# Adding and norming the experts' output earlier in an attention layer, its additions in halves, and zeros written by ScalarE

## The chip, the cores and the metric

The kernel runs on one core of a Trainium2 chip. A core has four engines that compute: TensorE (PE, matrix products into PSUM), VectorE (DVE), ScalarE (ACT, activation functions) and GpSimd (POOL). SyncE (SP) issues most of the transfers. Each engine works through its own queue in order, and semaphores tie the queues together. The metric is device time in microseconds (us); less is better.

## The reference

The whole program is a stack of eight layers on an input of 8 sequences of 512 positions by 256 features. Each layer is added to the residual stream as a normed output of a normed input:

```python
x = x + _layernorm(_L1_ffn_ref(_layernorm(x, axis=-1), ...), axis=-1)
x = x + _layernorm(_L2_attn_ref(_layernorm(x, axis=-1), ...), axis=-1)
```

The fourth layer, `_L1_ffn_ref`, is a mixture of 48 experts whose weighted outputs are scatter-added into one array. The fifth, `_L2_attn_ref`, is the third mixer of the stack and the place of the change. It is causal attention with 16 heads of 16 features, with a Silu on its three projections and q and k scaled by their norms:

```python
def _L2_attn_ref(x, Wq, Wk, Wv, Wo, q_scale, k_scale):
    q = jax.nn.silu(x @ Wq.T); k = jax.nn.silu(x @ Wk.T); v = jax.nn.silu(x @ Wv.T)
    ...
    r_q = jnp.linalg.norm(q, axis=-1, keepdims=True)
    r_k = jnp.linalg.norm(k, axis=-1, keepdims=True)
    q_dir = q / (r_q + EPS)
    k_dir = k / (r_k + EPS)
    scores = jnp.einsum('bhnd,bhmd->bhnm', q_dir, k_dir)
    scores = scores * (r_q * sq) * (jnp.swapaxes(r_k, -2, -1) * sk)
    scores = jnp.where(mask, scores, -jnp.inf)
    probs = jax.nn.softmax(scores, axis=-1)
    out = jnp.einsum('bhnm,bhmd->bhnd', probs, v)
    return out.transpose(0, 2, 1, 3).reshape(B, N, D) @ Wo.T
```

## The kernel before

The residual stream X stays in SBUF for the whole program, as a tile of 128 partitions by 4 blocks of 256 for each sequence. Everything is in 32-bit floats. A scheduler places the instructions, within each engine's queue, by the order of the program and by when it expects each to be ready. So an instruction can stand in its queue earlier than its place in the source.

The third mixer is `l2_attn`. It works on quads: a quad is four heads of one sequence, so a sequence has four. The main loop takes one turn for each of the 32 quads. A turn has two halves. In the first, `maxima` makes the scores S of the next quad (L1386) and DVE takes the greatest of each row (L1391, the group `junk`). These become one more column of q through a transpose (`ptm`) and an addition (L1400). In the second half, `weigh` makes the transposed scores T of this quad (L1421), ScalarE takes their Exp (L1424, into `PT`), POOL sets the upper triangle of the diagonal block to zero (L1426, `affine_select`, called the causal fill below), and PE multiplies by v (L1411, `o`). At the end `strip` transposes the q of the quad after next (`ptq`), and ScalarE and DVE copy it by turns into `qz`. One DVE copy (`OS`, L1435) and `spread` bring the output back into `O`.

Two further pieces of work hang on the sequences. `finish(b-1)` multiplies by Wo (L190), norms the product (`add_norm`, L164 on) and adds it to X; it is issued in the first turn of the next sequence. `front(b+1)` prepares the next sequence and is a generator which the loop advances by steps, four in each of the first two turns and up to twelve in the later ones. Its steps are, in this order:

- `late`: it loads the experts' output of that sequence from DRAM (`yl`, L1263), takes statistics on DVE, norms it on ScalarE (L177, `yn`) and adds it to X on POOL (L179, one addition of 128 x 1024);
- the norm of X (`lnst`, `lnmv`, `xn` L133), its transposes (`pxT`, L146; copied to `xT`, L148) and the first of four projections: q and k (`pqk`, L1317), v (`pv`, L1324), their Silus (L1321, L1327), the squares on POOL (L1330) and their sums on DVE (L1331);
- the second, third and fourth projection, one for each step;
- the norms of q and k: a chain of small DVE operations (L90 to L96, L1335 to L1341) whose result is `f`;
- the scaling of q and k by `f` on POOL (L1345, four instructions);
- four transposes of k (`ptk`, L1359) with their copies to `KT` (L1351).

Before the loop, front 0 runs by itself, and `maxima` of the first quad follows it. Several tiles hold zeros in places that are never written again: `qkp` (128 x 4096), `va` and `qz` (128 x 2048) and `mx` (128 x 512), each in two buffers. POOL writes them at the beginning (L1301 to L1306), with minus one and one in two narrow columns.

Silu and Exp belong to different tables of ScalarE. A change from one to the other is an instruction of its own in the trace (ACT_TABLE_LOAD). The tiles `yl` and `xn` share one buffer of the pool `s1`, so a load of `yl` can only start once the previous `xn` has been transposed. The PSUM pool for projections and transposes has two buffers, that for S and T has five.

## Time and profile before

| | us |
|---|---|
| median of 3 runs | 5200.95 (5196.74 to 5203.29) |
| profiled execution | 5193.12 |
| its span, first to last instruction | 5191.4 |
| third mixer, about | 2005 to 3085 |
| one of its sequences | 132.5 |

Inside the mixer, the engines' idle time before some groups of one sequence (window 2272 to 2404.5), with what ended it:

| group | idle before it, us | ended by |
|---|---|---|
| PE o, L1411 | 5.7 | POOL causal fill |
| PE pxT, L146 | 3.8 | DVE xn |
| PE S, L1386 | 2.7 | DVE maxima, ACT and DVE qz |
| PE ptk, L1359 | 1.7 | POOL scaling of q and k |
| PE T, L1421 | 1.7 | ACT Exp |

A timeline row has the start, the length (both in us), the engine, the line, the operation with output and inputs, the shape and the count; a bracket tells how long the engine stood idle before it and what ended that. A matrix product in 32-bit floats shows as two records. In a row of groups the numbers after the bar are busy time and the mean in ns, then the idle time before the group.

### The profile page before, as it was taken

What the parts mean: (1) busy time and instruction counts of PE and PEld (TensorE: products, weight loads), DVE (VectorE), ACT (ScalarE), POOL (GpSimd) and SP (SyncE); (2) the same over time, 40 slices, a digit from 0 to 9 for tenths busy, and PEclk for the clock granted to TensorE, in tenths of its full rate; (3) what the DMA queues carried; (4) which work ended last, traced back from release to release, by engine and by line L of the source; (5) the groups of instructions that cost most, each with busy time, mean ns of one, the idle gap of its engine ahead of it and who ended that gap; (6) DMA issues with size and microseconds to landing.
All of it is one profiled execution on the core that took longest, in us unless ns stands there. A gap on an engine that the chain in (4) does not pass through costs nothing.

```text
span 5191.4 us, 56559 instructions
## 1 busy us (share of the span) xinstructions
PE 4407.5 (85%) x18804; PEld 2700.6 (52%) x18804; DVE 3047.7 (59%) x8229; ACT 1928.3 (37%) x3817; POOL 1865.3 (36%) x1201
## 2 busy tenths in 40 slices
PE   8745789999983996988888899988888888899998
PEld 3334675565552894544444455533333333368885
DVE  7999646466687113555555653357778877761115
ACT  5401323434341332433333333355555555321112
POOL 0001213444342343111111110057889887803331
PEclk9876899999996997999999999999999999899999
DMA  4397411000001893000000000011111111126763
GB/s 113 80 208 176 132 47 48 5 5 9 5 17 42 225 253 97 5 5 5 5 5 5 1 20 1 0 43 42 45 45 49 45 43 43 47 80 216 227 214 101
DMA packets 401528, 357.89 MB, mean 69 GB/s; under 512 B 209394, under 2 KB 334020, under 8 KB 400676
## 3 DMA queue, kind: packets, MB, share of 16 engines
q1 hardware_dynamic: 373236, 305.83, 21.2%
q0 software_dynamic: 16320, 31.65, 2.2%
q10 hardware_dynamic: 11680, 16.80, 1.0%
q8 instruction: 149, 2.44, 0.2%
q14 instruction: 143, 1.17, 0.1%
HBM read 287.87 MB, written 66.09 MB: 68 GB/s over the span
## 4 chain that ended last, share of the span: by engine, by line
PE 34%; DVE 18%; issue 6%; POOL 5%; ACT 3%; DMA 1%; DVEq 0%; POOLq 0%; ACTq 0%; SPq 0%
DVE h L1706 7%; PE gb L1785 4%; PE T L1421 4%; PE h L1240 3%; DVE junk L1391 3%; PE g L1534 3%; PE y L1677 3%; PE yb L1799 2%; DVE dB L1652 2%; PE py L190 2%; PE pc L1599 2%; PE y L1251 2%; POOL h L1709 2%; PE o L1411 1%; PE pi L1585 1%
## 5 line engine op out<-in xcount | busy, mean ns | idle before, releaser
L1709 POOL TENSOR_TENSOR h<-h,C 128x1024 f32<-128x1024 f32 x256 | 596.2, 2357 | 178.2 <-DVE h L1706 140.0
L1677 PE MATMUL y<-h,C 128*128 128x512 f32 x1024 | 530.9, 659 | 104.6 <-POOL h L1709 104.6
L1706 DVE TENSOR_TENSOR_SCAN h<-dA,dB 128x512 f32<-128x512 f32 x512 | 589.4, 1204 | 29.4 <-ACT dA L1703 11.7
L1703 ACT ACTIVATE dA<-dl,A 128x512 f32<-128x512 f32 x512 | 352.5, 691 | 411.4 <-DVE h L1706 410.8
L935 POOL TENSOR_SCALAR p<-p,rs 128x128 f32<-128x128 f32 (+3 forms) x256 | 276.3, 1088 | 385.6 <-DVE rs L934 226.0
L1677 PEld LDWEIGHTS y<-h,C 128*128 128x128 f32 x1024 | 201.0, 207 | 410.9 <-issue 222.0
L1424 ACT ACTIVATE PT<-T 128x256 f32<-128x256 f32 (+3 forms) x512 | 208.5, 438 | 416.4 <-PE T L1421 409.8
L179 POOL TENSOR_TENSOR X<-X,yn 128x1024 f32<-128x1024 f32 x64 | 151.2, 2363 | 559.8 <-ACT yn L177 483.2
L1386 PE MATMUL S<-KT,qz 128*128 128x512 f32 (+3 forms) x1024 | 321.2, 453 | 22.4 <-DVE mx L1391 8.7
L1421 PE MATMUL T<-qz,KT 128*128 128x512 f32 (+3 forms) x1024 | 320.4, 445 | 12.0 <-ACT PT L1424 9.3
L1426 POOL TENSOR_SCALAR_AFFINE_SELECT PT<-PT 128x512 f32<-128x512 f32 x128 | 81.1, 637 | 609.8 <-ACT PT L1424 609.8
L1657 POOL TENSOR_TENSOR dB<-du,B 128x2048 f32<-128x2048 f32 x64 | 289.8, 4529 | 0.1
L1391 DVE CUSTOM_DVE_ANT_0 junk<-S,mask 128x256 f32<-128x256 f32 (+3 forms) x512 | 251.4, 491 | 61.9 <-PE S L1386 4.9
L1785 PE MATMUL gb<-xbT,w_b 128*128 128x256 f32 (+1 forms) x1472 | 255.3, 332 | 1.0 <-ACT ts L1989 0.6
L1386 PEld LDWEIGHTS S<-KT,qz 128*128 128x128 f32 x1024 | 180.4, 191 | 142.4 <-DVE mx L1391 30.7
L1652 DVE TENSOR_TENSOR dB<-du,pb 128x2048 f32<-128x2048 f32 x64 | 145.5, 2275 | 170.2 <-PE pb L1649 120.3
L1785 PEld LDWEIGHTS gb<-xbT,w_b 128*128 128x128 f32 x1472 | 230.2, 191 | 23.1 <-ACT ts L1989 0.8
L1791 DVE TENSOR_TENSOR hTb<-sb,gb 128x512 f32<-128x512 f32 x71 | 48.9, 688 | 325.3 <-PE gb L1785 325.3
L1421 PEld LDWEIGHTS T<-qz,KT 128*128 128x128 f32 x1024 | 169.1, 191 | 132.4 <-issue 66.5
L933 ACT ACTIVATE p<-p,nm 128x128 f32<-128x128 f32 (+3 forms) x256 | 143.8, 563 | 198.8 <-DVE nm L929 193.5
L1245 ACT ACTIVATE hT<-h,w_l_ffn 128x128 f32<-128x128 f32 x384 | 109.8, 368 | 220.3 <-PE h L1240 220.3
L1240 PE MATMUL h<-xgT,w 128*128 128x128 f32 x1536 | 185.0, 279 | 0.0
(506 smaller groups left out, 9132.7 us busy)
## 6 DMA issues: line engine op xcount, KB each, us to landing
w_b<-l3f_w SPq DMA_DIRECT2D x138, 512.0 KB
w<-l1f_w SPq DMA_DIRECT2D x48, 1024.0 KB
C<-xdd SPq DMA_DIRECT2D x128, 256.0 KB
B<-xdd SPq DMA_DIRECT2D x64, 256.0 KB
w<-l1f_w SPq DMA_DIRECT2D x48, 256.0 KB
toep<-l0fd SPq DMA_DIRECT2D x32, 320.0 KB
X<-x SPq DMA_DIRECT2D x16, 512.0 KB
toep<-l0fd SPq DMA_DIRECT2D x32, 256.0 KB
```

The costliest lines, as they stand in the source:

```text
L935: nc.gpsimd.tensor_scalar(p[:, 0:n], p[:, 0:n], rs, None, ALU.mult)
L1240: nc.tensor.matmul(ph[:, j, :], lhsT=w1[:, s, c, m * P:(m + 1) * P], rhs=xgT[:, c, :], start=(c == 0), stop=(c == 1))
L1386: nc.tensor.matmul(ps[:, 0:n], lhsT=QZ[:, j, qt * P:n], rhs=KT[:, g, 0:n], start=True, stop=True)
L1391: nc.vector.tensor_tensor_reduce(out=junk[:, 0:n], in0=tiles[j][:, 0:n], in1=mask[:, L - n:L], scale=1.0, scalar=-3.0e38, op0=ALU.add, op1 ...
L1421: nc.tensor.matmul(ps[:, 0:n], lhsT=KT[:, g, kt * P:(kt + 1) * P], rhs=QZ[:, j, kt * P:L], start=True, stop=True)
L1652: nc.vector.tensor_tensor(dB, du, pb[:, None, :].to_broadcast([P, 4, L]), ALU.mult)
L1657: nc.gpsimd.tensor_tensor(dB, du, B[:, None, :].to_broadcast([P, 4, L]), ALU.mult)
L1677: nc.tensor.matmul(py[2 * j + c], lhsT=K.ident, rhs=h[:, c, :], start=False, stop=(n == NS - 1))
L1703: nc.scalar.activation(dA, dl[:, c, :], AF.Exp, scale=A[:, c, n:n + 1])
L1706: nc.vector.tensor_tensor_scan(hs[-1][:, c % 2, :], dA, dB[:, c, :], 0.0, ALU.mult, ALU.add)
L1709: nc.gpsimd.tensor_tensor(h, h, C[:, None, :].to_broadcast([P, 2, L]), ALU.mult)
L1785: nc.tensor.matmul(ps[:, q, :], lhsT=ww[:, k, (c + q) * P:(c + q + 1) * P], rhs=xT[:, k, :], start=(k == 0), stop=(k == 1))
```

## The change

- `add_norm`, `project_out` and `late` can split the addition to X into parts; the third mixer uses two, each over half of the blocks.
- `front` yields once more, between the norm of X and its transposes. All eight fronts are made at the beginning. A new helper `norm_of` runs a front's first two steps, the addition of the experts' output and the norm. It is called for sequence b+2 in the last turn of sequence b; for sequence 1 behind `f` of front 0.
- The steps that the loop takes in each turn stay as they were in number, so with two of them gone ahead, all four projections fall into the first turn, and `f`, the scaling and two transposes of k into the second.
- The zeros are written by ScalarE, as an Identity with scale 0 of one column of the identity matrix, broadcast along the row. Buffer set 0 is done before front 0; set 1 behind the last Silu of front 0. The columns of minus one and one stay on POOL.
- `tc.issue_after(x)` keeps the instructions of its block behind x on x's own engine.

```diff
-    def add_norm(self, b, ys, pool, tag="yn", halves=()):
+    def add_norm(self, b, ys, pool, tag="yn", halves=(), parts=1):
...
-        nc.gpsimd.tensor_tensor(self.X[b], self.X[b], t, ALU.add)
+        m = NT // parts
+        for n in range(0, NT, m):
+            x = self.X[b][:, n:n + m, :]
+            nc.gpsimd.tensor_tensor(x, x, t[:, n:n + m, :], ALU.add)
...
-        K.add_norm(b, [y[:, n, :] for n in range(NT)], pool)
+        K.add_norm(b, [y[:, n, :] for n in range(NT)], pool, parts=2)
...
-        for j in range(2):
-            nc.gpsimd.memset(qkp[j], 0.0)
+        def padding(j):
+            for t in (qkp, va, qz, mx):
+                n = 1
+                for d in t[j].shape[1:]:
+                    n *= d
+                names = " ".join("abc"[:len(t[j].shape) - 1])
+                nc.scalar.activation(
+                    t[j].rearrange(f"p {names} -> p ({names})"),
+                    K.ident[:, 0:1].to_broadcast([P, n]), AF.Identity, scale=0.0)
             nc.gpsimd.memset(qkp[j][:, :, 16:32, 16:17], -1.0)
-            nc.gpsimd.memset(qz[j], 0.0)
-            nc.gpsimd.memset(mx[j], 0.0)
-            nc.gpsimd.memset(va[j], 0.0)
             nc.gpsimd.memset(va[j][:, :, :, 16:17], 1.0)

         def front(b, res):
             QKP, VA = qkp[b % 2], va[b % 2]
             K.late(b, s1)
             yield
-            xT = K.norm_T(b, s1, pmm, "mm")
+            xn = K.norm(b, s1)
+            yield
+            xT = K.norm_T(b, s1, pmm, "mm", xn=xn)
...
-                nc.scalar.activation(
+                res["v"] = nc.scalar.activation(
                     VA[:, n, :, 0:16], pv.rearrange("p (h d) -> p h d", h=16), AF.Silu)
...
-            nc.vector.tensor_tensor(
+            res["f"] = nc.vector.tensor_tensor(
                 f, f, row[:, None, :].to_broadcast([P, NT, 32]), ALU.mult)
...
-                b, [(OT[:, k, :], wo[:, k, :]) for k in range(2)], pmm, "mm", s1, leave=True)
+                b, [(OT[:, k, :], wo[:, k, :]) for k in range(2)], pmm, "mm", s1, leave=True, parts=2)
...
-        for _ in front(0, res[0]):
+        fronts = [front(b, res[b]) for b in range(NB)]
+        def norm_of(b):
+            if b < NB:
+                for _ in range(2):
+                    next(fronts[b])
+        padding(0)
+        for _ in fronts[0]:
             pass
+        with tc.issue_after(res[0]["v"].ins):
+            padding(1)
+        with tc.issue_after(res[0]["f"].ins):
+            norm_of(1)
...
-            if g == 0:
-                nxt = front(b + 1, res[b + 1]) if b + 1 < NB else iter(())
+            nxt = fronts[b + 1] if b + 1 < NB else iter(())
...
             for _ in range(4 if g < 2 else 12):
                 next(nxt, None)
+            if g == 3:
+                norm_of(b + 2)
             done[i] = weigh(b, g, made.pop(i), lambda: strip(i + 2))
```

More of the change, by code (lines that the diff above doesn't have):

```diff
@@ L178, in add_norm, with project_out @@
                 t[:, n, :], ys[n], AF.Identity, bias=nb[:, n:n + 1], scale=r[:, n:n + 1])
-        nc.gpsimd.tensor_tensor(self.X[b], self.X[b], t, ALU.add)
-    def project_out(self, b, chunks, psum, ptag, pool, tag="yn", leave=False):
+        m = NT // parts
+        for n in range(0, NT, m):
+            x = self.X[b][:, n:n + m, :]
+            nc.gpsimd.tensor_tensor(x, x, t[:, n:n + m, :], ALU.add)
+    def project_out(self, b, chunks, psum, ptag, pool, tag="yn", leave=False, parts=1):
         nc = self.nc
@@ L194, in project_out @@
             halves.append(ps)
-        self.add_norm(b, ys, pool, tag, halves if leave else ())
+        self.add_norm(b, ys, pool, tag, halves if leave else (), parts)
 def load_l0_attn(K):
```

## The prediction

> **What bounds the kernel now.** First the page: TensorE (PE) is busy most of the span, but that is a mean over eight layers. The edits lie in the third mixer and in the helper its input goes through.

> ```profile
> PE 4407.5 (85%) x18804; PEld 2700.6 (52%) x18804; DVE 3047.7 (59%) x8229; ACT 1928.3 (37%) x3817; POOL 1865.3 (36%) x1201
> ```

> Then the windows of the mixer (about 2005 to 3085 us). Its sequences repeat every 132.5 us. One such window (columns: window, length, then busy us and count of PE, PEld, DVE, ACT, POOL, clock, DMA):

> ```profile
> 2269.00:2402.00 133.00, 117.33 (x516) 64.84 (x515) 73.92 (x270) 51.90 (x105) 22.96 (x26) 0.95 0.02 5
> ```

> PE is the bound, with 15 us of gaps. The timeline of PE tells where they lie:

> ```profile
> 2343.35 1.98 PE L1421 MATMUL T<-qz,KT 128*128 128x512 f32 x4
> ...
> 2359.00 1.02 PE L1421 MATMUL T<-qz,KT 128*128 128x128 f32 x6 [0.34 <-ACT PT L1424]
> 2361.75 0.64 PE L1411 MATMUL o<-PT,va 128*32 128x256 f32 x8 [1.73 <-POOL PT L1426]
> 2366.29 0.66 PE L1411 MATMUL o<-PT,va 128*32 128x128 f32 x8 [3.89 <-POOL PT L1426]
> 2370.77 2.19 PE L146 MATMUL pxT<-C,xn 128*128 128x128 f32 x8 [3.83 <-DVE xn L133]
> ...
> 2383.89 1.12 PE L1386 MATMUL S<-KT,qz 128*128 128x512 f32 x2
> ...
> 2415.53 1.12 PE L1386 MATMUL S<-KT,qz 128*128 128x512 f32 x2 [0.26 <-ACT qz L1374]
> ```

> Taking the first S product of a turn as its start, the four turns of a sequence last 51.2, 31.6, 25.6 and 24.0 us (2332.69, 2383.89, 2415.53; then by the period from 2283.09, 2308.68). The last turn carries no front and is dense. The first turn carries the finish, the late addition and most of a front: its second half (T products on) is 40.5 us, 2343.35 to 2383.89. In it POOL's causal fills stand behind two whole additions to X (2358.76 and 2363.30, 2.35 us each), and the front's transposes wait for POOL X, then 4.6 us of DVE statistics. The second turn holds the fourth projection; its Silu falls among Exps:

> ```profile
> 2397.09 1.28 ACT L1321 ACT_TABLE_LOAD   x1
> 2398.64 0.60 ACT L1321 ACTIVATE qkp<-pqk 128x512 f32<-128x512 f32 x1 [0.27 <-PE pqk L1317]
> 2399.26 1.28 ACT L1424 ACT_TABLE_LOAD   x1
> 2400.55 0.60 ACT L1424 ACTIVATE PT<-T 128x512 f32<-128x512 f32 x1
> ```

> Last the beginning of the mixer, where nothing covers a wait:

> ```profile
> 2010.54 10.40 DVE L118 TENSOR_SCALAR onv<-onmv 128x4 f32<-128x4 f32 x1
> 2020.98 0.17 DVE L90 TENSOR_SCALAR ony<-onv 128x4 int32<-128x4 int32 x1
> ```

> A four-element instruction shown as 10.4 us ends as POOL's last large memset does (2019.12 + 1.80).

> **The change, part by part.** The built order of the changed kernel's instructions gives the queues; durations are the trace's.

> *Start.* Six large memsets and two small leave POOL. ScalarE's zeros of buffer set 0 cost, by the nearest long row,

> ```profile
> L1604 ACT ACTIVATE u<-u 128x2048 f32<-128x2048 f32 x8 | 15.3, 1912 | 0.1
> ```

> 1.91 twice, 3.6 for 4096 elements (1.91 plus 2048 at 0.83 ns, the slope between the 128- and 512-wide Exps) and 0.6: 8.0 us. They can run from 2005.1, when the scatter has landed as for the mask memset, to 2013.1. Behind them on ACT stands yn; its scale is ready at 2013.2 (onv at 2010.5 plus the 2.6 us chain), so they are covered, barely. Gain 10.2. Of X in halves only one addition and two statistics (1.9 us) follow yn instead of 3.9: 2.0 more. The Silu load no longer waits for the second yl (2038.56; free at 2035.4): 2.8. Sequence 1's addition and norm leave the middle of front 0: first Silu to the end of f took 19.5, and takes 3 projections at 2.67 (8.0), Silu, square and sum 2.4, and the undisturbed chain 6.1, together 16.5: 3.0. Set 1's zeros (8.0 again) lie on ACT while DVE and POOL make f and scale qkp (about 10 us). Given back: that yn (2.1) is now ahead of the first S, and the norm's pieces among the first maxima (1.8). Start: 18.0 − 3.9 = **14 us gained**. If the broadcast read made ACT half as fast, both sets would stick out by some 8 and 4: 2 gained. I take 14: L1604 has the same form.

> *First turn.* late(b+2) and its norm are written in the last quad, but the built order puts them right after front b+1's projections; late's SP load still waits for the transposes to free xn, so its position on SP is unchanged. It lands 3.7 us later; behind the DVE instruction that waits for it stand only sums of squares not needed for 15 us. All four projections now lie among the T products. With 0 at 2343.35: as before until the finish's products end at 8.45; transposes, then xT at 11.9. ACT has the finish's scale at 12.3 (0.8 sooner, no yl statistics between), and then runs without a gap: yn 2.05, eight table loads 10.3, four Silu pairs 3.5, ten Exps 3.5, the qz copy 0.6. S can begin at about **32.5**, against 40.5 with three projections. PE's own work there is 29.7, so ACT becomes this stretch's bound, by some 3 us. The halved adds and the fills on POOL are each ready before PE asks. Gain 8.1.

> [...] The row above shows the next instruction 1.29 us after the load's start. [...]

> *Second turn.* Its projection and four loads go, and PE work falls by 2.1. But f's DVE chain, once in an idle stretch, moves in among the maxima, where DVE is the pace (junk every 0.845 us). Small operations fit into the 0.22 us between an accumulator read and the next junk (O's products do today), so I price seven chain steps and three products at about 0.05, the reciprocal 0.7, L1338 0.4, OS 0.5, four statistics 0.14 each: some 2.8, with half a microsecond of late start 3.3. For late's halved adds on POOL, meeting DVE products with two SBUF inputs (one such met today took 0.89 instead of 0.16, at 2043.39), 1.5 more. S half 12.2 + 4.8 = 17.0. The T half like that of the third turn, 13.0, with one transpose fewer and 0.6 of waiting for POOL's qkp: 13.2. Sum 30.2, against 31.6: gain 1.4. Third turn: one transpose fewer, 0.4. The ends for DVE: nothing extra, or all at full busy time (chain 4.5, OS 0.7, statistics 1.65, both adds blocking 2.35: 9.2).

> *Sum.* Six sequences with finish and front: 6 × (8.1 + 1.4 + 0.4) = 59.4. Sequence 0 has no finish to gain from: its T half was already interleaved at 22.9 us and gets one more Silu with two loads and a yn (+4.0); second turn 32.1 to 30.0, third −0.4: net +1.5. Last sequence: nothing. 14 + 59.4 − 1.5 = **72 us**. The profiled execution (5193.12, span 5191.4) would be 5121; it lies 7.8 under the median of the runs, so 5200.95 − 72 = **5129**.

> **Rivals.**

> *DVE gives more back.* If moved steps count at their full busy time, each second turn costs 4.4 more; with sequence 0, 7 × 4.4 = 31: **5160**. For it: DVE is in order and PE's S buffers are five. Against: the O products that already ride there free.

> *Interleaved Silus stall PE (slower).* The second turn today is 31.6 against 25.6 with 1.7 more PE work: 4.3 us lost for one interleaved projection. If each of four costs that, the first turn is 57.2 (24.3 bare, 4.5 finish, 1.0 transposes, 10.3 projections, 17.2 stalls), the sequence 57.2 + 30.2 + 25.2 + 24.0 = 136.6, 4.1 worse; six of them +25, sequence 0 about +15, start −14: +26, **5227**. It decides once the first turn's T half exceeds 42 us. Against: sequence 0's first turn interleaves three with only 0.8 us over its PE work, and part of the 4.3 is waiting for qkp's scaling.

> *Only the start gains*: the turns cancel, 5200.95 − 14 = **5187**. *The change doesn't do what it says*: zeros or halves move but the scheduler keeps the waits, **5199**; the built order speaks against it.

> **How the numbers follow.** Main case 0.62 (its own range 5105 to 5150, from the DVE ends), DVE 0.18, start only 0.07, nothing 0.04, slower 0.09. About 0.2% (10 us) can be told from no change. Faster: 0.62 + 0.18 + 0.07 = 0.87; same 0.04; slower 0.09. The range 5100 to 5186 holds the first two cases and leaves out about 0.2.

> **What would show it.** Right: no 10-us onv; first S about 14 us earlier; PE without 3.9-us gaps before o and pxT; ACT nearly solid in the first turn's T half, eight loads at 1.28; period about 122.5. Wrong: table loads followed by idle ACT, S halves of second turns beyond 17 us, or PE waiting for Silu more than 3 us per sequence.

## The result and the profile after

| | before | changed |
|---|---|---|
| median of the runs shown, us | 5202.12 (5196.74 to 5203.87, 4 runs) | 5108.95 (5105.01 to 5111.53, 4 runs) |
| profiled execution, us (span) | 5193.12 (5191.4) | 5105.01 (5103.3) |
| third mixer, first load of `yl` to the load of `wd`, us | 1083.1 | 994.4 |

The ratio of the times is 0.9822, with a 95% interval of 0.9805 to 0.9839: some 93 us less. In the two profiled executions it is 88.1, and the mixer alone is 88.7 shorter; the layers ahead of it ended 3.8 later in the second execution and those behind took 3.1 less. The code there is the same in both, and in the profiles of the kernels below the mixer's first load lies anywhere from 2004.2 to 2018.2, so both are read as drift. The medians differ by more because the profiled execution before lay 9 us under its median and the changed one 4.

Times of turns below run from the first S product of one turn to that of the next, as in the prediction. Read along the whole mixer they are:

| | before | changed |
|---|---|---|
| first `yl` load to the first S | 63.4 | 46.9 |
| to the second S (the turns begin) | 78.7 | 64.3 |
| sequence 0: its four turns | 35.7, 32.1, 25.4, 24.0 | 38.8, 28.0, 24.9, 24.4 |
| sequences 1 to 6: first turn (mean) | 51.5 | 42.55 |
| second turn (mean) | 31.6 | 29.0 |
| third and fourth turn | 25.5, 24.0 | 25.05, 24.0 |
| last sequence: two turns with a next S | 30.4, 24.3 | 29.9, 24.0 |

The 88.7 us are 14.4 of start, 1.1 in sequence 0, 6 × 12.1 = 72.6 in the six like sequences and 0.5 at the end.

The page's busy times of the changed kernel barely differ from before; only the span does:

```profile
PE 4394.7 (86%) x18804; PEld 2694.8 (53%) x18804; DVE 3045.6 (60%) x8229; ACT 1958.5 (38%) x3835; POOL 1854.5 (36%) x1209
```

ACT has gained 30 us of work (zeros and table loads) and the span is 88 shorter. PE has lost 12.8 us of busy time with the same 18804 matmuls; that is a clue to which the text comes back.

The start, in the timeline of DVE, with the four-element instruction that took 10.40 us before:

```profile
2014.34 0.24 DVE L118 TENSOR_SCALAR onv<-onmv 128x4 f32<-128x4 f32 x1
```

and in that of ACT, the zeros ahead of the first scaling:

```profile
2008.88 3.62 ACT L1310 ACTIVATE qkp<-C 128x4096 f32<-128x4096 f32 x1 [7.18 <-DMA out_d<-yw,iT]
2012.40 1.89 ACT L1310 ACTIVATE va<-C 128x2048 f32<-128x2048 f32 x1
2014.20 1.89 ACT L1310 ACTIVATE qz<-C 128x2048 f32<-128x2048 f32 x1
2016.00 0.61 ACT L1310 ACTIVATE mx<-C 128x512 f32<-128x512 f32 x1
2017.04 1.09 ACT L177 ACTIVATE yn<-yl,onb,ony 128x256 f32<-128x256 f32 x2 [0.42 <-issue]
```

The zeros end at 2016.61 and the scaling follows at 2017.04, when its scale has just been made: covered, with nothing to spare.

The first turn, in the timeline of PE (start, length, what; in brackets the idle time ahead and what ended it):

```profile
2320.73 1.98 PE L1432 MATMUL T<-qz,KT 128*128 128x512 f32 x4
...
2331.34 1.98 PE L1328 MATMUL pqk<-w_l_attn,xT 128*128 128x512 f32 x4
...
2335.40 1.06 PE L1422 MATMUL o<-PT,va 128*32 128x512 f32 x8
...
2347.09 1.98 PE L1328 MATMUL pqk<-w_l_attn,xT 128*128 128x512 f32 x4
...
2352.56 1.12 PE L1397 MATMUL S<-KT,qz 128*128 128x512 f32 x2 [1.47 <-ACT qz L1385]
```

From the first T product to the next S are 31.8 us, where it was 40.5 with a projection fewer. The gaps of 1.73, 3.89 and 3.83 us ahead of o and of the transposes are gone; the only long one left is the 1.47 ahead of S. ACT in the same stretch:

```profile
2333.03 2.07 ACT L177 ACTIVATE yn<-yn,onb,ony 128x256 f32<-128x256 f32 x4 [0.89 <-DVE onb L170]
2335.12 1.28 ACT L1332 ACT_TABLE_LOAD   x1
2336.41 0.60 ACT L1332 ACTIVATE qkp<-pqk 128x512 f32<-128x512 f32 x1
2336.91 0.38 ACT L1338 ACTIVATE va<-pv 128x256 f32<-128x256 f32 x1
2337.30 1.28 ACT L1435 ACT_TABLE_LOAD   x1
2338.60 0.88 ACT L1435 ACTIVATE PT<-T 128x384 f32<-128x384 f32 x2
...
2351.95 0.56 ACT L1385 COPY qz<-ptq 32x512 f32<-32x512 f32 x1
```

The Silu starts 1.29 after its load does, the Exp 1.30 after its own. Eight loads stand here, ACT has no idle time from 2333.03 to 2352.5, and its last piece is the copy to qz for which S waits the 1.47 us. So ACT ends last in this stretch, 1.4 us behind PE, which is busy for 30.4 of the 31.8.

What the prediction had not looked at is the row of the granted clock. By windows (window, length, then busy time and count of PE, PEld, DVE, ACT and POOL, the granted PE clock, DMA share, GB/s), first of the kernel before, in the gaps of its first turn:

```profile
2363.50:2370.80 7.30, 0.69 (x9) 0.24 (x9) 4.67 (x24) 0.37 (x3) 2.73 (x2) 0.50 0.00 0
2370.80:2376.00 5.20, 5.17 (x12) 2.90 (x13) 0.88 (x3) 2.46 (x3) 0.00 (x0) 0.50 0.34 89
```

then of a whole sequence of the changed one:

```profile
2188.10:2309.00 120.90, 113.64 (x514) 62.87 (x513) 76.16 (x266) 54.17 (x106) 23.48 (x29) 1.00 0.02 5
```

Before, the clock is at half in and behind the gaps, 0.50 in both windows, and the front's transposes and first projection take longer: eight transposes 2.19 us and the first q and k product 3.55, in the changed kernel 0.60 for each four and 1.98. Over sequences 1 to 6, each taken from its first S to that of the next sequence, PE is busy for 116.7 us on the mean before and for 113.9 in the changed kernel, with the same matmuls. So of the 12.1 us won per sequence 9.2 are idle time of PE that is gone, and about 2.8 are the same work done at a higher clock (by sequence 0.94 to 0.96 before, 0.99 to 1.00 in the changed kernel). That the waits are what lowered the clock is tested in the last experiment.

### The profile page after: what moved, and what is told of

The parts are those of the page before. It is cut to its first block, busy times and chain, and to the rows that moved or that the text cites. A ratio compares the mean times of both kernels' runs of the same rounds, so it can differ in the third digit from the quotient of the medians.

```text
span 5103.3 us, 56570 instructions
## 1 busy us (share of the span) xinstructions
PE 4394.7 (86%) x18804; PEld 2694.8 (53%) x18804; DVE 3045.6 (60%) x8229; ACT 1958.5 (38%) x3835; POOL 1854.5 (36%) x1209
## 4 chain that ended last, share of the span: by engine, by line
PE 37%; DVE 18%; issue 4%; POOL 4%; ACT 3%; DMA 1%; DVEq 0%; POOLq 0%; ACTq 0%; SPq 0%
DVE h L1730 7%; PE T L1432 5%; PE gb L1809 4%; DVE junk L1402 3%; PE h L1243 3%; PE g L1558 3%; PE y L1701 3%; PE yb L1823 2%; PE py L193 2%; DVE dB L1676 2%; PE pc L1623 2%; PE y L1254 2%; POOL h L1733 2%; PE o L1422 2%; PE pi L1609 1%
## 5 line engine op out<-in xcount | busy, mean ns | idle before, releaser
L1730 DVE TENSOR_TENSOR_SCAN h<-dA,dB 128x512 f32<-128x512 f32 x512 | 589.0, 1203 | 29.4 <-ACT dA L1727 11.7
L182 POOL TENSOR_TENSOR X<-X,yn 128x1024 f32<-128x1024 f32 (+1 forms) x80 | 154.1, 1932 | 590.3 <-ACT yn L177 529.3
```

The source lines that it names most:

```text
L1730: nc.vector.tensor_tensor_scan(hs[-1][:, c % 2, :], dA, dB[:, c, :], 0.0, ALU.mult, ALU.add)
```

## Experiments

Medians are set against the changed kernel's 5108.95 us; each ratio is against the kernel before in the same set of runs. The first three each undo one part.

**The early addition and norm undone**

```diff
             xn = K.norm(b, s1)
-            yield
...
-        with tc.issue_after(res[0]["f"].ins):
-            norm_of(1)
...
-            if g == 3:
-                norm_of(b + 2)
```

> The changed kernel with the early addition and norm undone: both are again the first steps of a front, in the first turn, and the fourth projection falls into the second turn. Zeros by ScalarE and halved additions stay. Theory (the early norm and the regrouped projections carry most of the gain, the start carries about 15 us): the start gains 12 to 15, the halves about 2 us per sequence in the first turn, so 20 to 30 us under the kernel before, about 5175. Rival (the halved additions, by letting the causal fills through, carry the first turn's gain): 70 us or more under the kernel before, below 5135. First turns should stay above 48 us by the theory, near 44 by the rival.

Measured: 5172.43 us, ratio 0.9956 (0.9939 to 0.9973), 63 above the changed kernel. First turns are at 49.9 on the mean again (51.5 before), second turns at 31.64. So the place of this work carries the first and second turns; the halves alone bring 1.6 per first turn. This kernel takes the gathering of the projections back too; the fourth experiment separates the two.

**Additions to X in one piece**

```diff
-        K.add_norm(b, [y[:, n, :] for n in range(NT)], pool, parts=2)
+        K.add_norm(b, [y[:, n, :] for n in range(NT)], pool)
...
-... pmm, "mm", s1, leave=True, parts=2)
+... pmm, "mm", s1, leave=True)
```

> The changed kernel with each addition to X in one piece again. Theory (in the changed kernel the additions lie beside ScalarE's work, and only the start follows one directly): 2 to 5 us slower than the changed kernel, 5111 to 5114, with first turns still near 42.5. Rival (the halves are what keeps the causal fills on time): 3 us or more per sequence, 5130 or above.

Measured: 5116.89, ratio 0.9844 (0.9828 to 0.9861), 8 slower, where 2 to 5 were expected. The first S is 2.5 later and the second 3.7; first turns stay at 42.5, second ones grow by 0.35. With the late addition out of the way, halving the additions pays at the ends of the mixer, not in its turns.

**All zeros by GpSimd at the start**

```diff
-        padding(0)
...
-            padding(1)
+        for j in range(2):
+            nc.gpsimd.memset(qkp[j], 0.0)
...
+            nc.gpsimd.memset(va[j], 0.0)
```

> The changed kernel with all zeros written by POOL at the beginning again. Theory (the start's 10 us are DVE's four-element operation held up by POOL's memsets, and nothing else of the change helps there): 9 to 12 us slower than the changed kernel, about 5119, and the first onv again takes about 10 us. Rival (ScalarE's 8 us only replaced the wait, or the long onv is a recording artefact): within 3 us of the changed kernel.

Measured: 5123.3, ratio 0.9857 (0.9841 to 0.9874), 14.4 slower, more than the 9 to 12 that were expected. The same instruction in DVE's timeline is long again, and it ends as the last memset in POOL's does, at 2025.9:

```profile
2015.59 10.34 DVE L118 TENSOR_SCALAR onv<-onmv 128x4 f32<-128x4 f32 x1
...
2024.11 1.79 POOL L1308 MEMSET va<- 128x2048 f32 x1
```

The first S is 11.7 later. The long row comes and goes with the memsets on GpSimd, and it is no artefact of the recording, since the first S moves with it.

**The fourth projection back in the second turn**

```diff
-            for _ in range(4 if g < 2 else 12):
+            for _ in range((3, 5, 12, 12)[g]):
```

> The changed kernel with three front steps in the first turn and five in the second, so that only the early addition and norm differ from the old placing of the projections. Theory (the early norm opens the first turn; the fourth projection is worth little, since its two loads move with it): first turns near 38.5, second near 32 to 33, the whole within 10 us of the changed kernel on the slow side, 5109 to 5119. Rival (gathering the projections in the first turn is what pays): 4 us or more per sequence, 5135 or above.

Measured: 5132.9, ratio 0.9871 (0.9854 to 0.9887), close to the rival's 5135 and well above the theory's 5119. First turns fall to 38.9, but second turns are 34.3 to 37.2 (32.9 in sequence 6), above the 31.6 of before: f is made late and GpSimd scales behind it, as PE's timeline of this kernel shows:

```profile
2384.77 1.13 PE L1432 MATMUL T<-qz,KT 128*128 128x256 f32 x4 [1.03 <-ACT PT L1435]
...
2389.64 0.69 PE L1370 MATMUL ptk<-C,qkp 128*128 128x128 f32 x2 [2.77 <-POOL qkp L1356]
```

First and second turn together take 83.1 us before, 74.3 here and 71.6 in the changed kernel (means of sequences 1 to 6). So the early addition and norm bring 8.8 us per sequence and the gathering of the projections 2.8; with it the chain of f starts beside the first S of the second turn and not some 19 us later.

**No table loads**

```diff
-                nc.scalar.activation(qk, ps.rearrange(...), AF.Silu)
+                nc.scalar.activation(qk, ps.rearrange(...), AF.Identity)
...
-                    VA[:, n, :, 0:16], pv.rearrange(...), AF.Silu)
+                    VA[:, n, :, 0:16], pv.rearrange(...), AF.Identity)
```

> The Silu of the three projections q, k and v in the third mixer's fronts is left out (they are copied as they are), so that ScalarE has no table loads there; everything else is as in the changed kernel. Theory: eight loads of 1.28 us make ScalarE the bound of the first turn's second half by only 2 to 3 us over TensorE's own work, so without them the first turns fall from 42.5 to about 40, the first turn of sequence 0 falls by 1 to 3, later turns stay; the kernel is 15 to 20 us faster than the changed one (5109), about 5090 to 5095. [...] Second rival: TensorE's own work or the fills on GpSimd end last, and the loads are covered: first turns stay at 42 and the time at 5105 to 5110.

Measured: 5105.22, ratio 0.9815 (0.98 to 0.983): the second rival's numbers. But this run does not tell what it was made to tell. (The kernel leaves Silu out, so only its times are of use.) First turns are 43.1, and the timeline shows why: the scheduler put one of the late addition's scalings between the second and third projection on ACT, presumably since it no longer reckoned with the loads, and there ACT waited 3.66 us for `onb`. Only in sequence 6, which has no late addition, was the first turn 40.35 against 42.84. So the order had to be held:

```diff
-        for n in range(NT):
-            nc.scalar.activation(
+        with self.tc.issue_after(after) if after is not None else ExitStack():
+            for n in range(NT):
+                nc.scalar.activation(
...
-            K.late(b, s1)
+            K.late(b, s1, res_of[b - 1]["v"].ins if b > 1 else None)
```

> As the kernel without Silu (again the Silu of the three projections is left out; 5105.2 us, first turns 43.1), but the late addition's scalings on ScalarE are queued behind the last projection's copy, so that they no longer stand between the projections. Theory: without the loads the first turn's second half is bound by TensorE's own 30.4 us of busy time, so first turns are 40 to 41, 1.5 to 2.5 below the changed kernel's 42.5; the time is 5090 to 5098. Rival: the loads cost nothing, since TensorE and its waits for the late addition end last: first turns at 42 to 43, time at 5103 to 5110.

Measured: 5110.25, ratio 0.9829 (0.9814 to 0.9844). First turns are 41.2 to 41.6 (40.7 in sequence 6), a little above the 40 to 41 that were expected: without the eight loads a first turn is about 1.3 us shorter, out of 10.3 us of ACT's time. That is about as much as ACT had ended behind PE. The total missed the expected 5090 to 5098, since second turns grew to 28.5 to 31.0, and sequence 0's to 34.2; PE waits there several times 0.5 to 0.8 us for DVE. The order of the remaining work changed with the loads gone, so the total is no price of the loads; the first turns come nearer to one.

**f's chain behind the maxima**

```diff
+            if g == 1:
+                with tc.issue_after(made_at[0]):
+                    next(nxt, None)
-            for _ in range(4 if g < 2 else 12):
+            for _ in range((4, 1, 12, 12)[g]):
```

Here `made_at[0]` is the last addition to qz in `maxima`.

> The chain that makes f in the second turn stands behind the maxima's last addition to qz instead of among the maxima's reductions; the transposes of its K then fall into the third turn. Theory: what the chain costs among the maxima is the difference between the S halves of the second turns (15.0 us) and of the bare turns (about 12.2): second turns fall from 29.0 to about 26, third turns grow from 25.0 to about 26, about 2 us per sequence, about 5095. Rival: the 2.8 us come from the statistics of the late addition and the products of O that ride among the maxima, and the chain rides free: second turns stay at 28 to 29, and with the third turns a bit longer the time is 5109 to 5116.

Measured: 5115.65, ratio 0.9841 (0.9827 to 0.9854). Second turns fell by more than expected, to 24.5 (27.7 in sequence 6), and third turns rose to 31.5. Only in sequences 5 and 6 were third turns shorter, 27.0 and 27.8. What went wrong is in the timeline of POOL and PE:

```profile
2252.53 4.09 POOL L1356 TENSOR_TENSOR qkp<-qkp,f 128x512 f32<-128x512 f32 x4 [1.80 <-DVE f L1352]
...
2256.58 0.63 POOL L1440 TENSOR_SCALAR_AFFINE_SELECT PT<-PT 128x512 f32<-128x512 f32 x1
...
2257.26 0.65 PE L1425 MATMUL o<-PT,va 128*32 128x128 f32 x8 [2.92 <-POOL PT L1440]
...
2257.84 7.79 PE L1399 MATMUL S<-KT,qz 128*128 128x512 f32 x14
```

GpSimd scales q and k ahead of the last causal fill, PE waits 2.92 us for the fill, and the fourteen S products behind it take 7.79 us instead of the 5.42 of other turns. The windows of the same kernel give the reason for the second:

```profile
2253.00:2257.00 4.00, 1.12 (x2) 0.30 (x2) 2.08 (x4) 0.74 (x2) 4.00 (x5) 0.85 0.01 2
2257.00:2261.00 4.00, 3.74 (x12) 1.71 (x13) 1.39 (x3) 0.00 (x0) 0.21 (x1) 0.50 0.00 0
2261.00:2265.00 4.00, 4.00 (x10) 1.99 (x9) 2.32 (x7) 0.00 (x0) 0.00 (x0) 0.80 0.01 2
```

The clock falls to half during the wait and stays there for 6.8 us (0.15 × 4, 0.50 × 4 and 0.20 × 4, their sum over 0.5). A later kernel, with the scaling behind the fills, takes the wait away, and its clock is 1.00 there.

**The finish's scaling on VectorE as well**

```diff
         for n in range(NT):
-            nc.scalar.activation(
-                t[:, n, :], ys[n], AF.Identity, bias=nb[:, n:n + 1], scale=r[:, n:n + 1])
+            if halves:
+                nc.vector.tensor_scalar(
+                    t[:, n, :], ys[n], mv[:, n, 0:1], r[:, n:n + 1], ALU.subtract, ALU.mult)
...
```

> As the kernel with f's chain behind the maxima, and the finish's four scalings yn go from ScalarE (0.52 us each there) to VectorE as subtract and multiply. Theory: ScalarE is the bound of the first turn's second half, so 2.07 us less on it shorten each first turn by 1.5 to 2, from 42.5 to about 40.5 to 41, six times, 9 to 12 us less than the kernel with the chain behind the maxima, about 5083 if that one is at 5095. Rival: VectorE's 1.2 to 1.5 us for the same scalings stand ahead of the front's additions and squares, or the fills end last: first turns at 42 to 42.5 and the two kernels within 3 us.

This kernel also has f's chain behind the maxima, and is set against the last one. Measured: 5119.52, ratio 0.9843 (0.983 to 0.9857). First turns fell by only 0.75 (41.7), second turns rose by 1.6 (26.1). But ACT ended last here too, and had not become 2 us shorter, as the timelines of ACT and PE show:

```profile
2344.07 1.28 ACT L1442 ACT_TABLE_LOAD   x1 [0.79 <-PE T L1439]
...
2346.89 0.60 ACT L181 ACTIVATE yn<-yl,onb,ony 128x256 f32<-128x256 f32 x1 [0.87 <-issue]
```

```profile
2356.39 1.41 PE L1403 MATMUL S<-KT,qz 128*128 128x512 f32 x2 [2.13 <-ACT qz L1389]
```

In the changed order ACT stands idle for 0.79 and 0.87 us and takes one of the late addition's scalings, 0.60, ahead of the copy to qz: together 2.26 us, all of the 2.07 that was taken off. So this run does not tell what 2 us less on ACT are worth.

**The second sequence's norm not held behind f**

```diff
-        with tc.issue_after(res[0]["f"].ins):
-            norm_of(1)
...
-            for _ in range(4 if g < 2 else 12):
+            for _ in range((6 if i == 0 else 4) if g < 2 else 12):
```

> Only the second sequence's addition and norm are moved, from behind the first front into the first turn of sequence 0; all else is as in the changed kernel. Theory: behind the first front they cost about 2 to 4 us before the first and second S product (second S 64.3 us after the mixer's first load), but in the first turn of sequence 0 they cost more, since its transposes wait for the statistics there: second S 2 to 4 us earlier, first turn of sequence 0 longer by 4 to 8, in all 2 to 6 us slower than the changed kernel (5109), about 5112. Rival: its place does not matter, since the first turn of sequence 0 has idle time on every engine: the time stays at 5107 to 5110, or falls by what the second S gains, to 5105.

Measured: 5115.08, ratio 0.9838 (0.9823 to 0.9853), 6 slower, but not in the way that was expected. The first turn of sequence 0 is the same (38.7). Nothing holding them back any more, the scheduler took the addition and norm back into the first front, and the first S came 4.3 later, the second 2.3. POOL's timeline shows an addition between two squares of the front:

```profile
2039.17 1.04 POOL L1341 TENSOR_TENSOR sq<-qkp 128x512 f32<-128x512 f32 x1
2040.17 1.26 POOL L182 TENSOR_TENSOR X<-X,yn 128x512 f32<-128x512 f32 x1
2042.03 1.04 POOL L1341 TENSOR_TENSOR sq<-qkp 128x512 f32<-128x512 f32 x1 [0.60 <-ACT qkp L1332]
```

So this run measures the fence itself: 4.3 us at the first S, of which 2.0 are given back by the second.

**f's chain behind the maxima, and the scaling behind the fills**

The edit is shown against the kernel with f's chain behind the maxima:

```diff
-            for _ in range((4, 1, 12, 12)[g]):
+            for _ in range((4, 0, 12, 12)[g]):
...
             done[i] = weigh(b, g, made.pop(i), lambda: strip(i + 2))
+            if g == 1:
+                with tc.issue_after(filled_at[0]):
+                    next(nxt, None)
```

> As the kernel with f's chain behind the maxima (5115.7 us, second turns 24.5, third turns 31.5), but GpSimd's scaling of q and k by f also stands behind the last causal fill of the second turn instead of ahead of it. Theory: the third turns grew there because TensorE waited 2.9 us for that fill behind the scaling, and then ran its S products at half clock; with the fill ahead, third turns fall to about 25.5 to 26.5 and second turns stay at 24.5, so that a sequence is 3 to 3.5 us shorter than in the changed kernel (5109): about 5085 to 5092. Rival: f's chain on VectorE still delays the third turn's maxima, or K's transposes in the third turn cost what the second turn gained: third turns at 28 or more, time at 5100 or above.

Measured: **5089.77** (5084.13 to 5095.6, 5 runs), ratio 0.9794 (0.978 to 0.9807): as expected, and the fastest version. No run of it was as slow as the fastest of the changed kernel (5105.01); the two were not timed in one set. Second turns are 24.5 and third turns 26.1 on the mean, 3.4 less per sequence together. In PE's timeline of this kernel the last o product has no wait, and the S products are at their 5.42:

```profile
2250.68 0.43 PE L1425 MATMUL o<-PT,va 128*32 128x128 f32 x8
...
2252.71 5.42 PE L1399 MATMUL S<-KT,qz 128*128 128x512 f32 x14
```

The clock stays at full speed from sequence 1 to the last sequence:

```profile
2190.00:2963.00 773.00, 743.07 (x3389) 417.75 (x3391) 488.62 (x1767) 347.88 (x692) 149.95 (x179) 1.00 0.02 4
```

The mixer takes 970.4 us from first load to `wd`, 23.9 less than in the changed kernel; the medians differ by 19.2.

**The gaps filled with idle work**

This asks whether the half clock really follows from the gaps. To the kernel whose late addition stands in the front again, matmuls are added that nobody reads:

```diff
+            yn = K.late(b, s1)
+            for src, count in (((yn, 6), (K.X[b], 5)) if b > 1 else ()):
+                pw = pmm.tile([P, L], F32, tag="mm", name=f"pw{b}_{count}")
+                for _ in range(count):
+                    nc.tensor.matmul(
+                        pw, lhsT=K.ident, rhs=src[:, 0:2, :].rearrange("p n d -> p (n d)"),
+                        start=True, stop=True)
```

> As the kernel with the early addition and norm undone (5172.4 us, first turns 49.5), with eleven 512-wide matmuls per front on TensorE whose result nobody reads: six when the late addition's scaling is done, five when the first half of X is added. They fill the 4.6 us before the last o products and most of the 3.1 us before the front's transposes. Theory: the idle stretches also cost TensorE its clock, which stays at half for some 5 us behind them: with them filled the clock is 1.00 throughout, the eight transposes of xn take 1.2 us instead of 1.97 and the first projection's four products 2.0 instead of 2.9, and the first turn is 0 to 1.5 shorter, although more work stands in it (the last o products now come behind the transposes, about 1.0). Rival: the half clock has another cause (the transfers or the load of all engines there): the same products stay at 1.97 and 2.9, and the first turn grows by 1 to 3 us.

Measured: one run of 5181.26 (5201.64 for the kernel before beside it). PE's timeline without the filling, then with it:

```profile
2356.48 1.97 PE L146 MATMUL pxT<-C,xn 128*128 128x128 f32 x8 [3.06 <-DVE xn L133]
2358.91 2.01 PE L1327 MATMUL pqk<-w_l_attn,xT 128*128 128x512 f32 x2 [0.46 <-ACT xT L148]
```

```profile
2355.86 7.11 PE L1324 MATMUL pw<-yn,C 128*128 128x512 f32 x12 [1.44 <-ACT yn L177]
2362.81 4.46 PE L1324 MATMUL pw<-X,C 128*128 128x512 f32 x10
2367.10 1.04 PE L146 MATMUL pxT<-C,xn 128*128 128x128 f32 x8
...
2368.61 1.98 PE L1334 MATMUL pqk<-w_l_attn,xT 128*128 128x512 f32 x4
```

The same eight transposes take 1.04 instead of 1.97, four projection products 1.98 for what took 2.01 for two. The transfer's burst lies on this work as before (a DMA share of 0.35 in a window around it in both kernels, with a clock of 0.61 in that window without the filling and 1.00 with it), so the transfer by itself is not what lowers the clock here; what changed is what PE did just before. The other part of the rival, the load of all engines, is not held apart in the same way. First turns themselves grew by 1.4 on the mean (51.2), because the filling was twice as long as meant: one 512-wide product is two matmuls of the trace, ten of which took 4.46 us at full clock, so the eleven took 11.6 us and not 5.5. And the clock was not 1.00 throughout: in four of the six sequences it was still at half for 3.4 us, in the first filling.

## Why the prediction came out as it did

The forecast was 5129 from a gain of 72; 93 were measured in medians and 88.7 in the mixer. The result lies inside the main case's own range of 5105 to 5150, but near its lower edge. The mechanism and its places held; the sizes of several terms did not. One by one:

- **Start, 18.0 − 3.9 = 14.** Measured 14.4 at the second S. The 10.2 for `onv` is 10.2 (10.40 to 0.24), the zeros are covered by a hair, as said, and undoing them costs 14.4 in all. The 2.0 for halves measured 2.5 at the first S, the 3.0 for the undisturbed chain 4.3. The 2.8 for the Silu load has no run of its own.
- **First turn, 8.1.** Measured 9.0: the stretch from T is 31.8 where 32.5 was put. ACT starts the finish's scaling 12.3 after T, as put, runs without a gap and ends last, as put. The margin, "by some 3 us", was mis-sized: it is 1.4. The ten Exps took 3.0 where 3.5 was put, and PE is busy 30.4 where 29.7 was put. So without the loads the stretch lost 1.3 us and no more. In one point the sum was lucky. Before, PE was busy 30.7 in this stretch with three projections; at those rates a fourth, at 2.67, would have made it 33.4, more than ACT's 32.5. That the clock would come back, and PE's work stay at 30.4 with it, is not argued anywhere in the prediction.
- **Eight table loads, 10.3.** The prediction took them from the row of the kernel before, 1.29 from a load's start to the next instruction, and came to 32.5 for the stretch; 31.8 was measured. In the changed kernel each of the eight loads takes 1.28, and the instruction behind it starts 1.29 to 1.30 after the load does, with no idle time of ACT between. The row was the right source.
- **Second turn, 1.4.** Measured 2.6. This is the term that was off by most: 17.0 for the S half, where the maxima end 15.1 after the first S. The T half, 13.9 where 13.2 was put, took back 0.7 of that. The 1.5 for GpSimd meeting DVE shows only as two steps of 0.65 and 0.60 us where 0.22 and 0.29 are usual, and the chain's steps fit into the pauses between maxima, as the timeline of DVE shows:

```profile
2357.43 0.68 DVE L1402 CUSTOM_DVE_ANT_0 junk<-S,mask 128x512 f32<-128x512 f32 x1
...
2358.03 0.28 DVE L95 TENSOR_TENSOR qknw<-qknw,qkny 128x128 f32<-128x128 f32 x1
2358.26 0.69 DVE L1402 CUSTOM_DVE_ANT_0 junk<-S,mask 128x512 f32<-128x512 f32 x1
...
2358.88 0.29 DVE L96 SCALAR_TENSOR_TENSOR qkny<-qknw,qkny 128x128 f32<-128x128 f32 x1
2359.10 0.69 DVE L1402 CUSTOM_DVE_ANT_0 junk<-S,mask 128x512 f32<-128x512 f32 x1
```

  The maxima come every 0.84 with a step in between, as without. It is not all free: with the chain behind them the maxima end at 12.9, so the chain among them costs 2.2; that this is its start before the first maximum, its reciprocal and its tail is argued from their rows, not shown apart.
- **Third turn, 0.4.** Measured 0.45.
- **Sequence 0, +1.5; last sequence, nothing.** Measured −1.1 and −0.5. The first turn was near (+3.1 against +4.0), the second gained 4.1 instead of 2.1, which is the mis-sized second turn again.

Added up, what was missed is 6 × 0.9 in first turns, 6 × 1.2 in second ones, 2.6 in sequence 0 and under 1 in the rest: 16 us. Of the rivals, DVE giving back more was wrong in sign, and Silus that stall PE by 4.3 each were not seen.

Left open: why second turns grew with the loads gone, what 2 us less on ACT would be worth in the first turn with the order held, and whether two more table loads per projection would begin to show.

## What to carry to other kernels

A wait of the matrix engine cost twice here: its own 2.92 us, and the S products behind it at half clock, 7.79 us where 5.42 is usual; look at the granted clock by windows before a gap is priced. Work that is not needed soon belongs behind the queue's last urgent instruction, and each queue it touches has to be looked at: the same chain was worth −3.4 or, in most sequences, +2.0 us, by whether GpSimd's scaling stood behind or ahead of one fill. And when an experiment takes work away, read the order first: a scheduler that plans with the missing cost moves other things into its place.

## What the runs showed of the hardware

```profile
2356.12:2359.51 3.39, 3.39 (x5) 1.33 (x5) 2.04 (x9) 1.59 (x7) 3.39 (x4) 0.50 0.00 0
2754.00:2770.00 16.00, 15.36 (x56) 7.50 (x57) 5.93 (x27) 5.84 (x14) 4.72 (x5) 1.00 0.10 33
```

The same wait did not always go with the same clock. Behind the 1.44 us the first filling took 7.11 us in four sequences, with 3.4 us at half clock, and 5.42 in two, at full clock. Behind the 2.92 us the fourteen S products took 7.12 us in sequence 0 and 7.79 to 8.10 in sequences 1 to 4, where 5.42 is usual. Behind the 1.47 us ahead of S in the changed kernel the clock stayed at 1.00 for the next 12 us. Twice, in sequences 2 and 6, the changed kernel was at half clock for 3.4 us in the second turn, 13 to 14 us after that wait, where the nearest wait was 0.66. What decides is not shown.

The broadcast source showed no cost on ScalarE: 2048 zeros from one column took 1.89 us where 2048 elements from a plain tile took 1.91.
